# Spreading the next batch's projections over three groups of the first attention in a two-layer decoder kernel

## The chip, the core and the metric

The kernel runs on one core of a Trainium2 chip. A core has TensorE (PE in the profile, its weight loads PEld), VectorE (DVE), ScalarE (ACT), GpSimd (POOL) and SyncE (SP), which here only issues DMAs. The metric is the device time of one execution in microseconds; the time given for a kernel is the median of its runs.

## The reference, cut to what matters

Two decoder layers over `x` of shape (4, 1024, 256), each a self-attention, a cross-attention to 77 context tokens and a feed-forward part, all with a layer norm before and a residual after. The part that matters here is the first self-attention (16 heads of 16, causal, with ALiBi):

```python
x = x + _L0_attn_ref(_layernorm(x), L0_attn_w_attn, L0_attn_w_proj)
...
qkv = x @ w_attn.T
att = einsum(q, k) / sqrt(16) + causal ALiBi bias
y = softmax(att) @ v
return y @ w_proj.T
```

Then follow the cross-attention `_L0_xattn_ref`, the quantised feed-forward `_L0_ffn_ref`, and the second layer.

## The kernel before, in words

The kernel is written as Python generators. Each `yield` ends a step, and `weave(a, na, b, nb)` interleaves two generators so that `na` steps of the one go with `nb` of the other; when one has ended, the rest of the other follows alone. This gives a program order. A list scheduler then places the instructions of each engine: it takes them by readiness and by this order, and may pull later ones forward. Tiles of a tag share a fixed number of buffers (`BUFS`, one where the tag is not named), and a tile waits until a buffer of its tag is released. PSUM has eight banks with fixed duties (`BANKS`): row-maximum matmuls (tag M) and projections (tag Q) share banks 2 and 3, scores (S) have 0 and 1.

The first attention of batch b is `A0(b, after)` (lines 470 to 493). It works through four groups of four heads. In each group the main steps are `a0_main` (20 steps): the scores of a key block against a pair of query blocks (line 401, from the stacks QS and KS in bf16 parts), exp on ScalarE (line 404), and, two steps later, P times V (line 413). Beside them runs a side generator. In groups 0 to 2 it is `nxt`, which loads the next group's stacks (`stacks`, lines 310 to 327, two buffers each of QS and KS) and computes that group's row maxima (`a0_max`, 38 steps, matmul in line 352, reduction on VectorE in line 357). In group 3 it is `after`.

`after` is the front of the next batch, `A0_front(b + 1)`: `qkv` (lines 264 to 308) of 18 steps, then the stacks and the 38 row-maximum steps of its first group. `qkv` loads the weights (`load_w`, lines 256 to 261, 768 KB each into WAh and WAl, one buffer each), and for each half of the 1024 tokens it normalises x on VectorE and GpSimd, transposes it (one step), forms Q and K (four steps, line 288, six matmuls of 512 columns each, split into bf16 parts on ScalarE, VectorE and GpSimd in lines 290 to 293, stored to DRAM as `dr` in lines 296 and 297) and V (four steps, line 303, six matmuls each). For the last batch `after` is the front of the second layer's attention, `A1_front(0)`, with the same 18 steps and its gates.

At the end of `A0` the output is projected, `proj_res` (lines 441 to 460), whose weights also use the buffer WAh. So do `prep_p0` (line 334), which splits that weight once, and `prep_a1`.

Outside, `schedule` (lines 1199 on) weaves A0 of batch b with a side of its own. For batch 0 that is the preparation of weights, in this order: `prep_x(0)`, `prep_p0`, `prep_x(1)`, `prep_f0`; the first eight steps of it go beside the first front. The staging tag `wst`, two buffers, serves all of these. For batches 1 to 3 the side is the cross-attention `XA` of batch b - 1 (two rounds u of heads), the feed-forward `F0` (tanh in line 727, lines 729, 733 and 740 on VectorE), and what is left of the preparation.

Where the 18 projection steps go is set by `GQ`, `NQ` and `NW` (lines 94 and 95): `take(after, 12)` is woven into the side of group 2, the other six stand at the head of group 3, and the side gets 25, 25, 38 and 38 steps for 20 main steps in groups 0 to 3.

## Time and profile before

| | us |
|---|---|
| median of three runs | 2407.63 |
| the runs | 2401.26 to 2417.06 |
| the profiled execution's own time | 2403.86 |
| its span | 2402.1 |
| first attention, first to last score matmul | 102 to 1269 |

The profile is one execution. Busy times of engines are given in us; a row of instructions has its count, its busy time and the mean of one in ns, and the idle time of the engine before it with what ended that. The granted clock of TensorE is given as a share of full speed, the DMA share is the mean busy share of the core's 16 DMA engines. Score matmuls of batch b start at 102, 334, 644 and 948 us.

### The profile page before, as it was taken

Reading aid. Unit: us, or ns where it says so; the run is one execution under the profiler, and the core shown is the slowest. Engines: PE = TensorE matmul, PEld = TensorE weight load, DVE = VectorE, ACT = ScalarE, POOL = GpSimd, SP = SyncE. Lnnn points to the kernel's source line nnn. Section 1 sums busy time; section 2 is a strip of 40 time slices with the busy share of each in tenths; the row PEclk is TensorE's granted clock in tenths of the full one; section 3 lists DMA queues with packets and bytes.
Section 4 is the critical chain, followed back from the end, with each engine's and each line's share of the span. In section 5 each row is a group of like instructions: output and inputs, shape, how many; then the busy total and the mean of one; then the engine's idle time right before and its main releaser. Section 6 shows DMA issues by size and latency. Waiting matters only on the chain.

```text
span 2402.1 us, 51405 instructions
## 1 busy us (share of the span) xinstructions
PE 2150.0 (90%) x19073; PEld 1520.1 (63%) x19110; DVE 1688.9 (70%) x3781; ACT 1638.8 (68%) x4173; POOL 1196.0 (50%) x1942
## 2 busy tenths in 40 slices
PE   6798999998999998899988988889988998899886
PEld 5454457755667655576656766567766767676676
DVE  4666657677666787776765667777866777777775
ACT  4365446676766676565778878987678877887542
POOL 7121303154331352412545458766866787775664
PEclk9899999999999999899989999999999999899997
DMA  8677331224751236222262224412341223542000
GB/s 256 190 206 212 117 90 44 63 57 115 230 143 49 62 105 194 73 73 49 73 188 50 71 71 138 140 38 56 99 116 38 56 80 115 104 99 71 10 10 18
DMA packets 182697, 238.45 MB, mean 99 GB/s; under 512 B 16198, under 2 KB 165846, under 8 KB 175958
## 3 DMA queue, kind: packets, MB, share of 16 engines
q1 hardware_dynamic: 182446, 235.15, 34.9%
q8 instruction: 151, 2.47, 0.4%
q14 instruction: 100, 0.82, 0.1%
HBM read 152.62 MB, written 82.21 MB: 98 GB/s over the span
## 4 chain that ended last, share of the span: by engine, by line
PE 60%; DVE 13%; DMA 8%; ACT 7%; POOL 7%; issue 3%; SPq 1%; POOLq 0%; another core or an unknown queue 0%; ACTq 0%; DVEq 0%
PE T L191 10%; PE W L191 8%; PE O L413 7%; PE Q L191 5%; PE O L927 5%; PE S L401 4%; PE M L352 4%; PE S L898 3%; DVE P L904 2%; DVE s_mt L357 2%; PE W L630 1%; DMA wst<-in_L_xattn_Wq 1%; DMA KS<-c_alk 1%; ACT P L906 1%; PE T L723 1%
## 5 line engine op out<-in xcount | busy, mean ns | idle before, releaser
L357 DVE TENSOR_REDUCE s_mt<-M 128x1 f32<-128x512 f32 (+3 forms) x608 | 386.2, 656 | 135.1 <-PE M L356 97.3
L404 ACT ACTIVATE P<-S 128x512 f32<-128x512 f32 (+1 forms) x640 | 342.0, 562 | 152.3 <-PE S L401 77.0
L906 ACT ACTIVATE P<-P,eps 128x1024 f32<-128x1024 f32 x320 | 343.9, 1080 | 55.5 <-DVE P L904 52.6
L904 DVE TENSOR_REDUCE P<-S 128x512 f32<-128x512 f32 (+1 forms) x480 | 284.8, 611 | 78.2 <-PE S L898 58.6
L352 PE MATMUL M<-KS,QS 108*128 108x512 bf16 (+3 forms) x768 | 225.7, 339 | 47.8 <-DVE s_mt L357 24.6
L898 PE MATMUL S<-QS,KS 96*128 96x256 bf16 (+1 forms) x1280 | 219.4, 270 | 36.6 <-DVE P L904 34.1
L191 PE MATMUL T<-R,xX 128*128 128x352 f32 (+1 forms) x1136 | 246.5, 331 | 4.0 <-ACT E L619 1.4
L401 PE MATMUL S<-QS,KS 110*128 110x256 bf16 (+1 forms) x1280 | 230.4, 267 | 14.7 <-ACT P L404 12.4
L413 PE MATMUL O<-P,V 128*32 128x256 f32 (+1 forms) x2560 | 239.4, 376 | 0.5 <-ACT ot L427 0.2
L622 POOL TENSOR_TENSOR E<-E,s_xsm 128x616 f32<-128x616 f32 x64 | 77.8, 1217 | 323.9 <-DVE s_xsm L620 270.8
L191 PEld LDWEIGHTS T<-R,xX 128*128 128x128 f32 x1136 | 182.9, 190 | 24.1 <-ACT E L619 5.4
L191 PE MATMUL W<-R,xph 128*128 128x256 f32 (+1 forms) x952 | 184.8, 292 | 6.5 <-DVE xpl L180 4.8
L909 POOL TENSOR_TENSOR P<-P,y 128x512 f32<-128x512 f32 x128 | 164.8, 1296 | 31.8 <-ACT y L871 17.0
L619 ACT ACTIVATE E<-T,s_xmx 128x77 f32<-128x77 f32 x512 | 159.3, 333 | 28.1 <-DVE s_xmx L616 26.0
L927 PE MATMUL O<-P,VsJ 128*32 128x128 f32 x3584 | 170.4, 286 | 4.8 <-ACT P L906 3.8
L898 PEld LDWEIGHTS <-KS 96*128 96x128 bf16 x1280 | 102.1, 99 | 110.6 <-issue 88.9
L401 PEld LDWEIGHTS <-KS 110*128 110x128 bf16 x1280 | 106.9, 99 | 102.5 <-issue 58.6
L191 PEld LDWEIGHTS W<-R,xph 128*128 128x128 f32 (+1 forms) x952 | 149.1, 192 | 17.7 <-DVE xpl L180 6.6
L352 PEld LDWEIGHTS <-QS 108*128 108x128 bf16 x768 | 68.1, 99 | 126.5 <-issue 99.2
L191 PE MATMUL W<-R,xpl 128*128 128x256 f32 (+2 forms) x476 | 139.5, 293 | 0.8 <-DVE xpl L180 0.8
L730 POOL TENSOR_TENSOR R<-wst 128x256 f32<-128x256 f32 x128 | 92.9, 736 | 86.0 <-DVE wst L729 80.9
L179 ACT ACTIVATE xph<-W 128x512 fp32r<-128x512 f32 (+2 forms) x180 | 79.1, 457 | 83.1 <-PE W L633 34.0
(351 smaller groups left out, 5662.6 us busy)
## 6 DMA issues: line engine op xcount, KB each, us to landing
QS<-dr SPq DMA_DIRECT2D x144, 192.0 KB
KS<-dr SPq DMA_DIRECT2D x72, 384.0 KB
dr<-qp SPq DMA_DIRECT2D x32, 768.0 KB
MD<-R SPq DMA_DIRECT2D x24, 616.0 KB
UD<-R SPq DMA_DIRECT2D x24, 512.0 KB
R<-MD SPq DMA_DIRECT2D x32, 308.0 KB
X<-in_x SPq DMA_DIRECT2D x16, 512.0 KB
dr<-qp SPq DMA_DIRECT2D x32, 256.0 KB
```

The lines of the kernel that those rows point to most:

```text
L191: nc.tensor.matmul(out, x, y, start=first and n == 0, stop=last and n == len(seq) - 1)
L352: nc.tensor.matmul(Sv[:, x, 0:w], QS[:108, i // 4, hh, i % 4 * 128 : i % 4 * 128 + 128], KS[:108, hh, k0:k1], start=x == 0, stop=not diag ...
L357: nc.vector.tensor_reduce(out, Sv[:, :, 0:w], AX.X, ALU.max)
L401: nc.tensor.matmul(S[:, e, 0:w], st[1][:110, hh, j * 128 : (j + 1) * 128], st[0][:110, q0 // 512, hh, q0 % 512 : q0 % 512 + w], start=e == ...
L404: nc.scalar.activation(P[:, 2 * p : 2 * p + 2, 256 - w :], S[:, :, 0:w], AF.Exp)
L413: nc.tensor.matmul(O[0][hh * 32 : hh * 32 + 32, o + o0 : o + 256], V[j // 4][:, j % 4, h * 17 : h * 17 + 32], P[:, hh, o0:], start=c % 2 = ...
L619: nc.scalar.activation(E[:, n * 77 : (n + 1) * 77], Sv[:, k, :], AF.Exp, bias=mx[:, n : n + 1], accum_out=sm[:, n : n + 1])
L898: nc.tensor.matmul(S[:, e, 0:w], st[r][1][:96, hh, j * 128 : (j + 1) * 128], st[r][0][:96, q0 // 512, hh, q0 % 512 : q0 % 512 + w], start= ...
L904: nc.vector.tensor_reduce(Pv, S[:, :, 0:w].unsqueeze(3), AX.X, ALU.max, apply_absolute_value=True)
L906: nc.scalar.activation(Pw, Pw, AF.Square, bias=self.eps1)
L909: nc.gpsimd.tensor_tensor(Pd, Pd, Ds[r, c][:, j - 2 * c], ALU.mult)
L927: nc.tensor.matmul(Oc[rows, o0 : o0 + 128], lhs, P[:, hh, c0 : c0 + 128], start=j == 2 * c and i == 2 * c, stop=fin and i == 2 * c + 1)
```

## The change

Each of the groups 0, 1 and 2 now takes six steps of `after` beside the 38 row-maximum steps, so that all 18 projection steps are done in the first three groups and group 3's side begins with the stacks and row maxima of the next batch. The side gets 30, 30, 30 and 25 steps for 20 main steps. Nothing that is computed changes.

```diff
-    GQ, NQ = (2, 2, 2, 2), (12, 12, 12, 12)
-    NW = ((25, 25, 38, 38),) * 4
+    NQ = 6
+    NW = (30, 30, 30, 25)
...
         for g in range(4):
             box = []
             side = nxt(g + 1, box) if g < 3 else after
-            if g == self.GQ[b]:
-                side = weave(side, 28, take(after, self.NQ[b]), self.NQ[b])
-            yield from weave(self.a0_main(st, V, y, g, O, pend), 20, side, self.NW[b][g])
+            if g < 3:
+                side = weave(side, 38, take(after, self.NQ), self.NQ)
+            yield from weave(self.a0_main(st, V, y, g, O, pend), 20, side, self.NW[g])
             if g < 3:
                 st = box[0]
```

## The prediction

> **What bounds the kernel now.** I read the page's busy table first, then the busy times stretch by stretch, then what TensorE waited for in the first attention, then two places of the timeline. The times below are of the profiled execution: 2403.86 us by its own time, 2402.1 us of it span; the median of the three timed runs is 2407.63 us, 3.8 us more.

> ```profile
> span 2402.1 us, 51405 instructions
> PE 2150.0 (90%) x19073; PEld 1520.1 (63%) x19110; DVE 1688.9 (70%) x3781; ACT 1638.8 (68%) x4173; POOL 1196.0 (50%) x1942
> ```

> TensorE (PE) carries the span; 252 us of it are idle. The first attention runs from 102 to 1269 us (first to last score matmul, L401); its batches 1 to 3 split at the first and last tanh of F0 (L727):

> ```profile
> core 0: us, PE busy (x) PEld busy (x) DVE busy (x) ACT busy (x) POOL busy (x), PEclk, DMA share, GB/s
> 60.00:75.00 15.00, 8.82 (x51) 6.37 (x51) 5.48 (x10) 4.54 (x10) 2.57 (x3) 0.80 1.06 316
> 102.00:334.00 232.00, 207.70 (x1675) 119.99 (x1673) 142.62 (x269) 131.75 (x276) 53.86 (x53) 0.93 0.57 167
> 334.00:509.00 175.00, 168.66 (x1423) 119.51 (x1422) 120.98 (x281) 110.01 (x407) 37.76 (x53) 0.99 0.24 57
> 509.00:582.00 73.00, 66.02 (x519) 38.36 (x526) 56.98 (x133) 58.51 (x127) 42.30 (x72) 1.00 0.24 74
> 582.00:644.00 62.00, 56.30 (x418) 37.75 (x416) 41.21 (x81) 38.56 (x78) 23.11 (x26) 0.92 0.69 208
> 644.00:842.00 198.00, 195.14 (x1555) 135.53 (x1556) 137.64 (x317) 126.93 (x445) 53.08 (x75) 1.00 0.37 98
> 842.00:923.00 81.00, 75.32 (x566) 44.55 (x573) 62.35 (x144) 60.19 (x133) 40.65 (x65) 0.96 0.35 98
> 948.00:1156.00 208.00, 191.53 (x1505) 131.52 (x1502) 149.26 (x344) 119.51 (x428) 61.13 (x85) 0.95 0.30 82
> 1156.00:1232.00 76.00, 67.61 (x501) 40.40 (x507) 59.11 (x136) 59.42 (x136) 39.34 (x66) 0.96 0.32 102
> 843.00:903.00 60.00, 55.76 (x435) 32.30 (x441) 52.09 (x118) 45.04 (x98) 32.05 (x52) 0.96 0.40 111
> ```

> Per row: PE, weight loads, VectorE (DVE), ScalarE, GpSimd (POOL), granted clock, DMA. The first halves, with XA beside the attention, are solid TensorE (334:509 idles 6.3 us, 644:842 2.9 us). The F0 stretches (509:582, 842:923, 1156:1232) have VectorE at 0.77 to 0.78 and idle 7.0, 5.7 and 8.4 us. Batch 0 (102:334) idles 24.3 us. At 60:75 the DMA engines are full. The waits of TensorE between 102 and 1269 us:

> ```profile
> PE M L352 <- DVE s_mt L357: 22.3, 42, 2.5
> PE M L352 <- DMA KS<-c_alk: 14.0, 4, 6.9
> PE S L401 <- ACT P L404: 12.4, 15, 3.1
> PE M L352 <- DVE yTl L180: 2.8, 4, 1.4
> ```

> Total us, times, longest. Row-maximum matmuls (M) wait for the reduction that frees their PSUM bank, or for the key stack (KS). Two timeline places, the start of the row maxima and the load of batch 1's projection weights:

> ```profile
> 72.38 0.37 PE L352 MATMUL M<-KS,QS 108*128 108x128 bf16 x2 [4.55 <-DMA KS<-dr]
> ```
> ```profile
> 120.06 0.89 SPq L259 DMA_DIRECT2D WAh<-wa  x1
> 126.55 1.24 SPq L260 DMA_DIRECT2D WAl<-wa  x1
> ```

> **The change part by part.** No instruction is added or removed; the two built programs hold the same numbers on every engine. What moves is one batch's 18 projection steps (96 matmuls, 16 transposes, their evacuations, 4 DMA stores, 2 loads of x, 2 of weights) and, because weights and scheduler follow, more than the diff shows.

> *1. The steps themselves.* Eight steps cost 1.39 us of TensorE and eight 0.76 us (six matmuls each, chain of waits at 844 and 911 us), two are transposes of about 1.2 us (8 by 0.15): 19.6 us a batch, 1.1 us a step. Twelve of 18 leave the second half of each attention: 13 us. They land where TensorE idles 1 to 4%, so they cost there what they save here. Net 0, if the second half really becomes shorter; item 4 asks that.

> *2. Start-up, +5 us.* Batch 1's weights load in group 0 now. In the built order SP issues WAl and WAh right after the fourth Wk load of the start-up (some 60 us), no longer at 120 and 127 us; the last QS pieces and the KS pieces of batch 0's first stack stand behind them on SP, and so does the next cross-attention weight load. 2 by 768 KB is 1.57 MB; at the 316 GB/s of 60:75, with the engines full, 5.0 us. The first row maximum already waits 4.55 us for KS, so nothing covers this. Bounds: 0 (if the weight preparation beside it ends later anyway) to +7 (two issues of 0.9 and 1.2 us waited out too). The old place gives nothing back: TensorE was 100% busy there.

> *3. Batch 0 loses its filler, 0 us.* WAh and WAl have one buffer. Batch 1's load now stands before prep_p0, which splits Wproj into the same buffers; so prep_p0 waits until batch 1's 18th step, holding both wst buffers, and prep_x(1) and prep_f0 wait behind it. In the built order prep_x(1)'s matmuls move from 87..164 to 213..289 us of accumulated TensorE work, prep_f0's from 166..196 to 290..331: into the last group of batch 0 and the first of batch 1. On POOL the V memset that waits for batch 0's last P.V (17.5 us at 328 us before) now has half of prep_x(1)'s subtractions behind it; TensorE has proj_res and scores beside them. XA's second round, which reads prep_x(1)'s result, stands 115 us of TensorE work behind it, so it is covered. What it costs: from 102 to about 240 us only the attention and its projections run. Bounds: -14 (all KS waits go, with less DMA beside the stacks) to +16: 140 us at the poorest TensorE share that 60 us of this phase show, 0.78 (927 to 987 us), instead of 102:334's 0.895 are 125.3/0.78 - 140 = +20.6, less 4.5 us, half of batch 0's 9.0 us of KS waits, which lighter DMA should give back. I take 0: attention alone keeps TensorE ahead of ScalarE (1.47 us of matmul a main step against 1.07 us of exp), and the KS waits shrink.

> *4. Second halves, +5 us.* With 20 main steps to 30, 30, 30, 25 side steps, not 25, 25, 38, 38, the side steps left over when a group's main steps are done are 14, 14, 14, 13 instead of 13, 13, 12, 6: in groups 2 and 3, where F0 runs, nine more, most of them row maxima without a score step beside them. Between the first and last tanh of F0 the built order has 24, 35, 30 row maxima before and 47, 46, 43 after; projection steps 10, 14, 13 before, 8, 7, 6.3 after. 47 more reductions by 0.635 us (386.2 us / 608) are +29.8 us of VectorE, 15.7 steps by 0.46 us (8 subtractions of 0.69, 4 of 0.68 in 18 steps) -7.2: +22.6 us in three stretches, 7.5 each. VectorE goes from 57.0, 62.4, 59.1 to about 64.5, 69.9, 66.6 us. The best it held over 60 us is 52.09 of 60 (843:903), 0.87: 74, 80, 77 us against 73, 81, 76. So on the mean it costs +1, in clumps more. Cutting both orders into pieces of 10 us of TensorE work and adding the longest engine of each (mean durations of the rows) gives 1229.8 us before and 1257.8 after for the phase: +28. Bounds: -8 (waits of M and Q on each other's banks, 2.8+2.6+2.5 us, vanish) to +28; taken near the mean's end, because engines slip against each other by more than 10 us and the number of row maxima that stand tightly behind one another does not change (181 and 182).

> *5. End of batch 3.* A1_front(0) ends at 1121 us of TensorE work, before 1125; the wait for its gates (2.1 us) may go: 0, bounds -2 to 0.

> Sum: +5 +0 +5 +0 = +10 us: 2413.9 us for the profiled execution, 2418 against the median. Bounds added up: -24 and +51.

> [...]

> **Rivals.** (a) *Faster*: the KS waits vanish, because each group starts with projections beside it and batch 0's DMA is lighter: -14 us at their four places, and the clock of 102:334 recovers from 0.93 (7% of 232 us, about half of it: -8), with the +5 of item 2: 2386.9, 2391 on the median. For: KS ended 14.0 us of waits. Against: the wait at 72 us grows. It decides if the KS waits left fall below 4 us. (b) *VectorE becomes the bound of the second halves*: item 4 at +28, with +5: 2436.9 plus clock 2, 2443. For: the counts of item 4. Against: 0.87 was reached beside TensorE at 0.93. (c) *Batch 0 starves*: item 3 at +16, with +5: 2425, 2429. For: KS waits of up to 6.9 us even with filler. Against: the step costs in item 3. (d) *Nothing changes*: TensorE is the bound and the order is immaterial: 2408; against it, item 2's queue.

> **How the numbers follow.** Forecast 0.48 (own range 2405 to 2434), (a) 0.13, (b) 0.14, (c) 0.13, (d) 0.12. From (a)'s 2391 to (b)'s 2443, which leave out half of each, some 0.86 lies inside; rounded: 2390 to 2444. About 1% (24 us; 2384 and 2432) is what a measurement of this kernel can tell from no change. Slower by over 1%: (b) 0.14, half of (c) 0.06, the forecast's upper end 0.08: 0.28. Faster: half of (a), 0.07. Within: 0.65.

> **What would show it.** Item 2: both weight loads near 60 us on SP, the first M at 77 to 79 us instead of 72.4. Item 3: no Wk loads between about 110 and 220 us; TensorE at 0.88 to 0.92 there. Item 4: VectorE at 0.85 or more in the F0 stretches, waits of M for L357 above 22.3 us. The forecast is wrong if the first M is on time, if TensorE falls under 0.85 in batch 0, or if the F0 stretches idle more than 30 us together.

## The result and the profile after

The changed kernel takes 2441.06 us (median of four runs, 2437.19 to 2448.28) against 2410.33 us for the kernel before in the same comparison: 1.0148 times as long, with a 95% interval of 1.012 to 1.0176. It is 31 us slower, where +10 was forecast and rival (b) stood at 2443. The profiled execution took 2440.09 us, 2438.3 of it span; the page's first lines:

```profile
span 2438.3 us, 51436 instructions
PE 2181.2 (89%) x19110; PEld 1529.5 (63%) x19110; DVE 1692.4 (69%) x3781; ACT 1641.0 (67%) x4173; POOL 1202.0 (49%) x1942
```

The span is 36.2 us longer, 5.5 more than the medians differ: each profile is one execution, and the one of the kernel before was among its shorter ones. TensorE (PE) idles 257.1 us of the span, 5.1 more than before, and is busy 31.1 us longer with the same matmuls. Of that, 10.5 us are TensorE at half clock, which the record shows as busy time (worked out from the granted clock over the busy time: 88.9 us lost before, 99.4 after). An estimated 4 us are records missing from the trace of before (37 matmuls of 512 columns): taking 37 such records out of the complete trace of after shortens its busy time by 3 to 5 us. The other 16 or so are busy time at the same clock. At full clock a record of each of the larger kinds is as long as before, within 2% (a P.V of 256 columns 391 ns on the mean in both traces, 397 over all clocks), but the records overlap less with their neighbours, so that together they cover more time: those wholly at full clock add up to 5443 us and cover 1967 before, 5432 and 1977 after. The stretches, in the columns shown before, first by batch (first score to first score), then the pieces inside:

```profile
core 0: us, PE busy (x) PEld busy (x) DVE busy (x) ACT busy (x) POOL busy (x), PEclk, DMA share, GB/s
104.10:318.70 214.60, 197.09 (x1593) 110.52 (x1592) 126.79 (x232) 120.23 (x249) 34.56 (x36) 0.94 0.41 112
318.70:660.10 341.40, 308.86 (x2452) 206.17 (x2452) 241.91 (x537) 218.88 (x638) 124.41 (x167) 0.98 0.43 121
660.10:984.20 324.10, 301.21 (x2356) 195.06 (x2355) 232.25 (x530) 209.35 (x615) 106.82 (x154) 0.95 0.41 116
984.20:1298.00 313.80, 292.38 (x2262) 187.72 (x2260) 207.39 (x490) 204.23 (x606) 111.28 (x174) 0.95 0.31 88
...
61.00:82.00 21.00, 17.19 (x70) 13.43 (x71) 10.57 (x21) 5.95 (x13) 2.58 (x3) 0.51 1.05 333
...
523.00:600.00 77.00, 71.23 (x527) 40.67 (x525) 66.49 (x157) 55.70 (x121) 33.95 (x50) 0.96 0.26 72
...
858.00:938.00 80.00, 74.08 (x560) 39.95 (x559) 64.39 (x151) 57.93 (x126) 31.68 (x48) 0.91 0.26 69
938.00:984.00 46.00, 36.54 (x289) 18.78 (x289) 40.56 (x87) 26.44 (x49) 12.93 (x14) 0.81 0.70 223
...
1172.00:1247.00 75.00, 67.84 (x500) 36.97 (x498) 60.56 (x141) 54.33 (x119) 32.41 (x49) 0.93 0.23 71
```

The batches took 231.6, 310.9, 303.9 and 320.6 us before. Batch 0 is 17.0 us shorter and batch 1 30.5 longer, because half of the weight preparation moved from the one to the other; together +13.5. Batch 2 is +20.2, batch 3 -6.8, the start +2.1, all behind the first attention +7.3. The F0 stretches, from first to last tanh 79.2, 80.6 and 75.8 us, are together 3 us longer than before (73.5, 82.0 and 77.0). What has grown in batch 2 is the stretch behind F0, 46 us at a clock of 0.81, partly because it holds more of the batch's matmuls (289 against 215); in the kernel before it was the row

```profile
923.00:948.00 25.00, 22.45 (x215) 11.99 (x212) 20.68 (x45) 17.39 (x33) 4.80 (x7) 0.93 0.85 268
```

Split into waits, clock and busy time at the same clock, batch 2's +20.2 us are +11.8, +6.9 and +1.5. In batches 0 and 1 together the +13.5 are +6.7, -0.6 and +7.4, and behind the first attention the +7.3 are -3.5, +0.7 and +10.1 (the last of the three parts with the missing records). So no one part carries all stretches.

The waits of TensorE over the first attention (104 to 1298 us; total us, times, longest):

```profile
PE M L352 <- DVE s_mt L357: 26.3, 50, 1.7
PE S L401 <- ACT P L404: 13.9, 17, 3.6
PE W L747 <- DVE xph L740: 12.3, 8, 3.2
...
PE M L352 <- DMA KS<-c_alk: 2.6, 1, 2.6
```

The waits of L747 for L740 were half as long in the kernel before (102 to 1269 us):

```profile
PE W L747 <- DVE xph L740: 6.1, 5, 1.7
```

The waits for KS fell from 14.0 to 2.6 us, below the 4 us at which rival (a) was to decide, and nothing of it arrived in the time. In their place are waits of up to 3.6 us, 0.5 to 1.5 us on the mean of a row, spread over many pairs: over the first attention TensorE idles 94.4 us, where it idled 83.7 before. What such waits do to the clock is seen behind F0 of batch 2, where the transposes of the last F0 tiles wait for VectorE (timeline, then the clock of the same place):

```profile
940.43 0.32 PE L352 MATMUL M<-KS,QS 108*128 108x384 bf16 x1 [0.55 <-DVE s_mt L357]
...
942.76 1.03 PE L747 MATMUL W<-identb,xph 128*128 128x128 bf16 x8 [1.95 <-DVE xph L740]
...
948.37 0.59 PE L352 MATMUL M<-KS,QS 108*128 108x256 bf16 x2 [1.04 <-DVE VsJ L384]
...
951.14 1.03 PE L747 MATMUL W<-identb,xph 128*128 128x128 bf16 x8 [1.97 <-DVE xph L740]
```
```profile
928.10:941.70 13.60, 11.48 (x95) 5.48 (x93) 11.70 (x24) 10.88 (x24) 5.21 (x8) 1.00 0.37 93
941.70:955.30 13.60, 9.01 (x47) 5.53 (x48) 10.04 (x28) 4.40 (x6) 1.30 (x2) 0.50 0.89 278
```

TensorE stands at half clock for 13.6 us, four windows of 3.41 us (the last section has these windows): its 9.0 us of busy time there, times the clock, are an estimated 4.5 us of work. The window before, up to 941.66 us, idles 1.85 us, in pieces of 0.45, 0.55 and 0.85 us, of which the last is the first part of the wait for L740. The next three idle 1.40, 1.04 and 1.97 us, the fourth 0.22 us, and behind that the clock is whole again. Last, the start-up. On SP the two weight loads stand ahead of the KS and QS pieces, and the first row maximum (M) comes at 75.11 us, not 72.38:

```profile
57.53 0.89 SPq L260 DMA_DIRECT2D WAl<-wa  x1
58.52 0.42 SPq L259 DMA_DIRECT2D WAh<-wa  x1
...
71.48 1.30 SPq L320 DMA_DIRECT2D KS<-dr  x2
```
```profile
75.11 0.58 PE L352 MATMUL M<-KS,QS 108*128 108x128 bf16 x4 [2.22 <-DMA QS<-dr]
```

### The profile page after: what moved, and what is told of

Read it like the earlier page. It is cut to its first block, busy times and chain, and to the rows that moved or that the text cites. A ratio compares the mean times of both kernels' runs of the same rounds, so it can differ in the third digit from the quotient of the medians.

```text
span 2438.3 us, 51436 instructions
## 1 busy us (share of the span) xinstructions
PE 2181.2 (89%) x19110; PEld 1529.5 (63%) x19110; DVE 1692.4 (69%) x3781; ACT 1641.0 (67%) x4173; POOL 1202.0 (49%) x1942
## 4 chain that ended last, share of the span: by engine, by line
PE 61%; DVE 14%; ACT 7%; DMA 7%; POOL 7%; issue 4%; SPq 1%; POOLq 0%; DVEq 0%; ACTq 0%
PE T L191 10%; PE W L191 8%; PE O L413 7%; PE O L927 5%; PE Q L191 5%; PE S L401 5%; PE M L352 4%; PE S L898 3%; DVE s_mt L357 3%; DVE P L904 2%; PE T L723 2%; DMA wst<-in_L_xattn_Wq 2%; PE W L630 1%; PE W L752 1%; ACT P L906 1%
## 5 line engine op out<-in xcount | busy, mean ns | idle before, releaser
L357 DVE TENSOR_REDUCE s_mt<-M 128x1 f32<-128x512 f32 (+3 forms) x608 | 387.9, 656 | 131.5 <-PE M L356 97.6
L404 ACT ACTIVATE P<-S 128x512 f32<-128x512 f32 (+1 forms) x640 | 339.3, 562 | 133.3 <-PE S L401 79.9
L352 PE MATMUL M<-KS,QS 108*128 108x512 bf16 (+3 forms) x768 | 228.3, 343 | 42.4 <-DVE s_mt L357 28.6
L401 PE MATMUL S<-QS,KS 110*128 110x256 bf16 (+1 forms) x1280 | 230.5, 267 | 18.7 <-ACT P L404 13.9
L927 PE MATMUL O<-P,VsJ 128*32 128x128 f32 x3584 | 176.6, 283 | 6.4 <-ACT P L906 5.0
L401 PEld LDWEIGHTS <-KS 110*128 110x128 bf16 x1280 | 105.9, 99 | 108.0 <-issue 64.9
L352 PEld LDWEIGHTS <-QS 108*128 108x128 bf16 x768 | 69.7, 101 | 118.7 <-issue 95.4
```

The costliest lines, as they stand in the source:

```text
L352: nc.tensor.matmul(Sv[:, x, 0:w], QS[:108, i // 4, hh, i % 4 * 128 : i % 4 * 128 + 128], KS[:108, hh, k0:k1], start=x == 0, stop=not diag ...
L357: nc.vector.tensor_reduce(out, Sv[:, :, 0:w], AX.X, ALU.max)
L401: nc.tensor.matmul(S[:, e, 0:w], st[1][:110, hh, j * 128 : (j + 1) * 128], st[0][:110, q0 // 512, hh, q0 % 512 : q0 % 512 + w], start=e == ...
L404: nc.scalar.activation(P[:, 2 * p : 2 * p + 2, 256 - w :], S[:, :, 0:w], AF.Exp)
L927: nc.tensor.matmul(Oc[rows, o0 : o0 + 128], lhs, P[:, hh, c0 : c0 + 128], start=j == 2 * c and i == 2 * c, stop=fin and i == 2 * c + 1)
```

## The experiments

Unless said otherwise five rounds were taken, and each ratio is to the kernel before in the same comparison.

**Runs 1 to 4: the one weight buffer, and single batches.** Theory Q puts the loss on `prep_p0`, which waits for batch 1's projections to release WAh and WAl; theory V on VectorE in the second halves. Runs 1 and 2 give `prep_p0` the buffers xph and xpl, in the changed kernel and in the kernel before:

```diff
-        self.wp0 = self.prep_w(self.i["L0_attn_w_proj"], 256, "wp0")
+        self.wp0 = self.prep_w(self.i["L0_attn_w_proj"], 256, "wp0", tags=("xph", "xpl"))
```

Runs 3 and 4 make the change only in batch 0, or only in batches 1 to 3 (`new = b in (0,)` or `(1, 2, 3)` chooses between the old and the new lines).

> The changed kernel, but prep_p0 splits Wproj into the buffers xph and xpl instead of WAh and WAl, so that it no longer waits for the last of batch 1's projection steps. Theory Q (the queue behind the one weight buffer): aligned by TensorE work done, the changed kernel loses about 14 us until the middle of batch 1, where the late prep_x(1) and prep_f0 run; with their own buffers they run in batch 0 again and these 14 us return: about 2427 us against 2441, ratio to the kernel before 1.006 to 1.010. Theory V (the second halves, VectorE and F0): the loss sits in the F0 stretches, so nothing returns: 2438 to 2444, ratio 1.013 to 1.016.

> Control: the kernel before with the same other buffers for prep_p0. There prep_p0 stands ahead of batch 1's weight load, so by both theories nothing waits that waited not before: 2405 to 2415 us, ratio 0.998 to 1.002.

> The change (six steps in each of groups 0 to 2, rates 30, 30, 30, 25) in batch 0 alone; batches 1 to 3 as before. Theory Q: the whole buffer queue is in here, so about 14 us of the 31 us: 2424, ratio 1.004 to 1.008. Theory V: batch 0 has no F0 beside it, so nothing: 2410, ratio 0.998 to 1.002.

> The change in batches 1 to 3 alone; batch 0 as before, so prep_p0 and prep_x(1) are on time. Theory Q alone: 2410 us, ratio 0.998 to 1.002. Theory V alone: the whole 31 us, 2441, ratio 1.013. If both hold, each with the part that the alignment by TensorE work shows (14 us by the middle of batch 1, 13 us in the F0 stretches of batches 2 and 3): about 2424, ratio 1.004 to 1.008.

Measured: run 1 2442.70 us (ratio 1.0129, 1.0096 to 1.0161), run 2 2416.31 (1.0039, 1.0017 to 1.006; just over the range expected, so the other buffers cost some 7 us by themselves), run 3 2453.28 (1.0179, 1.0148 to 1.0209), run 4 2438.50 (1.0117, 1.0088 to 1.0146). Run 1 does what Q says where Q says it, batches 0 and 1 by score boundaries:

```profile
106.30:342.50 236.20, 211.75 (x1680) 122.50 (x1679) 151.25 (x279) 130.68 (x276) 54.96 (x53) 0.92 0.56 157
342.50:654.20 311.70, 296.11 (x2355) 194.41 (x2352) 213.09 (x490) 206.43 (x609) 101.13 (x148) 0.97 0.32 88
654.20:990.10 335.90, 303.09 (x2369) 198.70 (x2368) 231.86 (x535) 210.01 (x615) 106.30 (x154) 0.94 0.42 114
```

Batches 0 and 1 together take 547.9 us, against 542.5 before and 556.0 in the changed kernel: 8 of the 13.5 us are back. But batch 2 now takes 335.9, 12 more than in the changed kernel, and the total has not moved. Q falls as the cause of the total. V's numbers fit runs 1 and 4, not run 3: the change in batch 0 alone costs 44 us, in batches 1 to 3 alone 30, in all four 31. The parts do not add up.

**Runs 5 to 8: rates, and VectorE in F0.** Run 5 is the changed kernel with `NW = (32, 32, 32, 32)`, run 6 the kernel before with `NW = ((24, 24, 36, 31),) * 4`. Runs 7 (before) and 8 (changed) shorten the reduction of F0:

```diff
-                nc.vector.tensor_reduce(a[:, 0:1], hp, AX.X, ALU.max, apply_absolute_value=True)
+                nc.vector.tensor_reduce(a[:, 0:1], hp[:, 0:64], AX.X, ALU.max, apply_absolute_value=True)
```

> The changed kernel with the rates (32, 32, 32, 32) in place of (30, 30, 30, 25): six projection steps in each of the first three groups as in the change, but the side steps left over when a group's main steps are done are 12, 12, 12, 6, near the 13, 13, 12, 6 of the kernel before. Theory T (the rates: longer tails of row maxima ahead of the next group's first scores, above all in the last group, 13 for 6): 2400 to 2418, the loss gone. Theory V (VectorE bounds the F0 stretches, since row maxima stand where projections stood): 2433 to 2445, as the changed kernel, since the row maxima stay there. Theory P (where the projection steps stand costs by itself, outside F0): 2433 to 2445 too; told from V by the light pair.

> The kernel before with the rates (24, 24, 36, 31) in place of (25, 25, 38, 38): the placement of the projection steps is the old one, but 14, 14, 14, 13 side steps are left over at the groups' ends, as in the change. Theory T: 2430 to 2445. Theories V and P: 2403 to 2416, the time before.

> The kernel before with F0's reduction for the abs max (L733, 1212 ns, 32 of them) over 64 of the 1024 columns: it leaves out the other 960 columns' part of that max. It takes about 1 us by 8 off VectorE in each F0 stretch and off the tail of each F0 tile. A control for the next run: 2385 to 2405 by every theory.

> The changed kernel with the same reduction over 64 of 1024 columns (the other columns are left out of the max). Theory V: VectorE in the F0 stretches is relieved by 8 us each, so this gains 15 to 24 us more than the control does, and stands 5 to 16 us above it. Theories T and P: it stands 25 to 35 us above the control, as the changed kernel stands above the kernel before.

Measured: run 5 2437.90 us (1.0124, 1.0103 to 1.0146), run 6 2434.38 (1.0106, 1.0088 to 1.0123), run 7 2397.39 (0.9952, 0.9937 to 0.9967), run 8 2440.32 (1.0135, 1.0117 to 1.0153). The old rates' tails do not save the changed kernel (run 5), and longer tails alone cost 26 us (run 6), so T holds one way and fails the other. Runs 7 and 8 tell most. The control gains 11 us, with F0 stretches 5 to 12 us shorter each; the changed kernel gains nothing, although its F0 stretches became 8 to 11 us shorter each, by the first and last tanh. The rows are of run 8, from within 2 us of its first and last tanh:

```profile
526.30:594.50 68.20, 62.02 (x449) 35.54 (x454) 55.72 (x148) 52.53 (x110) 34.19 (x50) 0.97 0.16 55
858.70:927.60 68.90, 62.49 (x465) 35.26 (x472) 56.42 (x147) 53.22 (x114) 34.11 (x50) 0.95 0.17 55
1176.40:1244.10 67.70, 61.17 (x457) 35.07 (x468) 55.67 (x146) 52.64 (x115) 34.47 (x50) 0.95 0.16 56
```

V expected 15 to 24 us more than the control's gain and got some 10 less. VectorE in F0 is not the bound of the changed kernel; that is also rival (b)'s mechanism. What was left is P, that the placement costs by itself, with run 6 (the old placement) against it.

**Runs 9 to 12: the crowded end of batch 2, and the clock by itself.** Runs 9 (changed), 10 (before) and 11 (changed, with run 1's buffers) move a weight preparation:

```diff
-    more = {1: K.prep_x(2), 2: chain(K.prep_a1(), K.prep_f1_up()), 3: K.prep_f1_down()}
+    more = {1: K.prep_x(2), 2: K.prep_a1(), 3: chain(K.prep_f1_up(), K.prep_f1_down())}
```

Run 12 (one execution) replaces the whole decoder by matmul blocks that wait for VectorE copies:

```python
for n in (12, 28):
    for k, v in ((1, 64), (1, 256), (1, 512), (2, 256), (2, 512), (3, 512), (4, 512)):
        for _ in range(16):
            ps = K.p("S")
            nc.tensor.matmul(ps[:, 0:w], K.identb, r[:, 0:w], start=True, stop=True)
            for _ in range(n):
                nc.tensor.matmul(ps, K.identb, base, start=True, stop=True)
            w, a = v, ps
            for x in range(k):
                r = K.t([128, 512], BF if x == k - 1 else F32, "P" if x == k - 1 else "E")
                nc.vector.tensor_scalar(r[:, 0:w], a[:, 0:w], 1.0, None, ALU.mult)
                a = r
```

> The changed kernel with the preparation of the second feed-forward's up weights moved from batch 2's side to batch 3's. In the stretch behind F0 of batch 2 (938 to 984 us of the changed kernel) VectorE is busy 40.7 of 46.1 us, some 20 of it with this preparation, TensorE idles 9.5 us and the clock is 0.81; before, that stretch took 25 us. Theory E (that crowded end holds about 14 of the 31 us): 2424 to 2432, the stretch ends in about 30 us. Theory D (the loss is spread over many short stalls that any other order also makes): 2434 to 2446, what is won there comes back elsewhere.

> The kernel before with the same move, as control. Theory E: 2400 to 2410, since this stretch idles only 2.6 us there. Theory D: 2412 to 2435, since any other order of this kernel loses.

> The changed kernel with both: the projection weights of batch 0's side in buffers of their own (as in the first run of this study, which brought batches 0 and 1 back to within 6 us of the kernel before) and the move of the up weights' preparation. If the losses are local and add up: 2412 to 2425. Theory D: 2434 to 2446.

> No decoder at all (zeros are written, everything is left out): blocks of 12, then of 28 bf16 matmuls of 512 columns, each block waiting for a chain of one to four VectorE copies of the block before, 16 blocks for each of seven chain lengths. Theory C (the granted clock is set by the idle share of windows of 3.41 us: half speed for the next window when about half of one was idle, and held there while more than about 0.15 is): blocks of 12 (2.6 us) with waits under 0.6 us run at 1.0, with waits over 1.2 us at 0.5 to 0.7; blocks of 28 (6 us) hold 1.0 up to waits of 1.3 us and fall to about 0.75 at 2 us and more. [...]

Measured: run 9 2424.68 us (1.0074, 1.0052 to 1.0097), run 10 2394.57 (0.9951, 0.9933 to 0.9969), run 11 2424.34 (1.0075, 1.0051 to 1.0099). The move gains 16 us in the changed kernel, as E says, but 11 in the kernel before, which E did not say: the two stay 30 us apart. E is no cause of the difference. Run 11 lies at the upper end of the range for losses that add up (2412 to 2425), but the buffers add nothing in it (run 11 against run 9), so the local losses do not add up. D, as written, falls too: run 10 is another order and is faster. Run 10 beats both kernels and computes the same. Runs 9 and 10 are the cleanest pair for where the time goes, both with all 19110 matmuls on record:

```profile
span 2423.2 us, 51456 instructions
PE 2167.8 (89%) x19110; PEld 1529.4 (63%) x19110; DVE 1695.0 (70%) x3781; ACT 1640.4 (68%) x4173; POOL 1200.9 (50%) x1942
```
```profile
span 2392.8 us, 51488 instructions
PE 2146.2 (90%) x19110; PEld 1517.3 (63%) x19110; DVE 1691.4 (71%) x3781; ACT 1639.0 (68%) x4173; POOL 1199.7 (50%) x1942
```

Run 9 is first, run 10 second. Idle of TensorE: 255.3 against 246.6, +8.7. Busy: +21.7. Busy time weighted with the granted clock is 2064.2 us in both, so all of that is the clock (103.6 us lost to it against 82.0): in this pair 9 us more of waits went with 22 us more lost to the clock. That the weighted time is the same is particular to this pair: in the six other traces that hold all 19110 matmuls, the changed kernel's among them, it lies between 2055.4 and 2081.8 us.

Run 12 has waits and clock without the decoder. Blocks of 28 matmuls, waits of 1.71 us, then of 2.17 us:

```profile
1062.00:1175.00 113.00, 89.87 (x406) 39.60 (x406) 20.93 (x42) 0.00 (x0) 1.00 0.00 0
1195.00:1337.00 142.00, 113.06 (x406) 45.16 (x404) 26.34 (x54) 0.00 (x0) 0.83 0.00 0
```

One more VectorE copy lengthens the wait by 0.46 us (30.3 against 23.9 us over 14 waits) and the period from 8.13 to 10.26 us, by 2.13. The rest, 1.67, is by an estimate one window of 3.41 us at half speed in each period: that costs 1.71, and the clock of 0.83 takes 1.74 from 10.26 us. Blocks of 12 do the same (4.67 to 6.82 us, clock 1.00 to 0.75). C is right on the step and on the long blocks (0.83 for about 0.75), wrong for short blocks with waits of 1.24 and 1.70 us, which stayed at 1.0 although 30 to 36% of the time was idle, while the long blocks at 0.83 idled 20% of theirs: the idle share of a whole stretch did not set its clock.

**Runs 13 to 16: other placements.** On run 10 as base, with the projection steps of groups 0, 1, 2 as `NQ` and the rest at the head of group 3:

```diff
-            if g == self.GQ[b]:
-                side = weave(side, 28, take(after, self.NQ[b]), self.NQ[b])
+            if g < 3 and self.NQ[g]:
+                side = weave(side, 28 if self.NQ[g] > 6 else 38, take(after, self.NQ[g]), self.NQ[g])
```

Run 13: `NQ = (0, 6, 6)`, run 14 `(0, 0, 18)`, run 15 `(6, 6, 0)`, run 16 `(0, 0, 6)`.

> On the tenth kernel of this study (2394.6): 0, 6, 6 projection steps in groups 0 to 2 and six at the head of group 3, rates 25, 30, 30, 38, so six steps stand one group earlier. Theory B (local balance: the sum over pieces of 10 us of TensorE work of the engine busiest in each, taken from the built orders, is 6 us higher, and 15 us higher went with 30 us before): 2404 to 2412. Theory L (the last group loses its projections; row maxima alone there): 2390 to 2402, since group 3 keeps its six.

> The same base with all 18 projection steps in group 2 and none in group 3, rates 25, 25, 43, 32. Theory B (the sum over pieces is 0.6 us lower): 2388 to 2400. Theory L: 2412 to 2427, since group 3 has no projection left, as in the change.

> The same base with 6, 6, 0 steps in groups 0 to 2 and six at the head of group 3, rates 30, 30, 25, 38. Theory B (the sum over pieces is 16 us higher; VectorE is the longest there where six steps went into group 0, beside the start and end of the cross-attention): 2417 to 2432. Theory L: 2392 to 2405.

> The same base, the other way: only six steps in group 2 and twelve at the head of group 3, rates 25, 25, 30, 43. Theory B (the sum over pieces is 6 us lower): 2380 to 2392. Theory L: 2385 to 2398. Both: no slower than the base.

Measured: 2461.80 us (1.0228, 1.0203 to 1.0254), 2428.59 (1.0086, 1.0062 to 1.0109), 2436.44 (1.0116, 1.0091 to 1.014) and 2433.27 (1.0104, 1.008 to 1.0129): 67, 34, 42 and 39 us above run 10. (Run 10 was measured in another comparison, whose kernel before took 1.7 us less.) B fails on run 13 (2404 to 2412 expected), 14 (2388 to 2400) and 16 (2380 to 2392) and misses run 15 by 4 us, so the sum over pieces is no measure of this either; L fails on 13, 15 and 16 and misses run 14 by 2 us. Even the opposite of the change, projections later than before, loses. In all four runs the rates change together with the placement, and rates alone cost 26 us in run 6: what placement alone costs is not separated.

All pairs that differ in the weave of the first attention alone, old placement and rates against others (the split is of the profiled executions, one of each kernel; what is left of the span's difference, 0 to 22 us, is TensorE records that overlap less at the same clock, and missing records. From run 10 to run 13, for one, the 2048 P.V of 256 columns take 394 and 395 ns on the mean, but cover 202.2 and 216.6 us):

| pair | difference of medians, us | idle of TensorE, us | lost to the clock, us |
|---|---|---|---|
| before, changed | +31 | +5.1 | +10.5 |
| the same, own buffers (runs 2, 1) | +26 | +6.5 | +17.7 |
| the same, light reduction (7, 8) | +43 | +18.3 | +9.3 |
| the same, preparation moved (10, 9) | +30 | +8.7 | +21.6 |
| before, runs 3, 4 (some batches) | +44, +30 | +16.9, +14.9 | +25.4, +8.8 |
| before, run 5 | +30 | +7.1 | +17.0 |
| before, run 6 (rates alone) | +26 | +4.6 | +18.3 |
| run 10, runs 13, 14, 15, 16 | +67, +34, +42, +39 | +19.4, +11.7, +17.6, +23.0 | +34.1, +18.1, +8.5, +4.6 |

Edits that leave this weave alone went the other way or cost little: run 2 +7, run 7 -11, run 10 -11.

The executions of one kernel differ in their clock. Over the 51 executions of the kernel before in the comparisons of runs 1 to 16 (2397.8 to 2425.4 us, mean granted clock 0.960 to 0.945) the time rises by 1.5 us for each 0.001 that the clock falls, with a correlation of -0.82. The mean of that clock is 0.954 in these, 0.952 in the four executions of the changed kernel, 0.958 in run 10 and 0.950 in run 9. By that slope the clock is worth an estimated 3 us of the 31 in the first pair and 12 of the 30 in the second, less in both than the split of single executions gives.

## Why the prediction was wrong, point by point

The step that failed is that the same instructions take TensorE the same time: item 1's "Net 0", with the clock left out of the sum. The sum's +10 is waits for other engines and queues. Measured were +5.1 us of idle time and +31.1 us of busy time in the profiled pair, +8.7 and +21.7 in the clean pair (runs 10 and 9). The second failure is item 4, whose +5 us stood in the wrong place. None of the prediction's own signs of being wrong appeared: the first M was late, TensorE was 0.92 busy in batch 0, and the three F0 stretches idle 18.9 us together, not over 30. The loss lay where no sign looked.

*Item 1, the steps, 0:* runs 9 and 10 do the same 2064.2 us of clock-weighted TensorE work with the steps in either place, but the kernel before and the changed one do not: 2061.2 and 2081.8 us, of which the missing records explain an estimated 4. So net 0 is not shown.

*Item 2, start-up, +5:* right in mechanism, the loads stand where forecast (57.5 and 58.5 us on SP), and the first M still waits for a DMA. The size was 2 to 3 us, within its bounds: the first M came 2.7 us later (77 to 79 was forecast, 75.1 measured), the first score 2.1. The wait itself became shorter (2.22 us against 4.55), while from 61 to 82 us the clock was 0.51, against 0.84 in the same stretch before; up to the first score TensorE idles 2.0 us less and loses 5.7 us more to the clock.

*Item 3, batch 0's filler, 0:* batch 0 itself did not starve (TensorE 0.93 busy from 110 to 220 us, where 0.88 to 0.92 was forecast, and no Wk load on SP from 90 to 260 us) and is shorter by the moved preparation; but batches 0 and 1 together lost 13.5 us, inside the bounds of -14 to +16 and far from the value taken. Run 1 gives 8 of it back by taking away the wait for WAh and WAl, and batch 2 then loses 12 more.

*Item 4, second halves, +5:* this step failed in place and size: batches 2 and 3 together are +13.4 us. F0 is only 3 us longer in the three stretches together; VectorE stood at 0.86, 0.80 and 0.81 there, not at 0.85 or more throughout, and lightening it (run 8) bought nothing. The waits of M for its reduction rose from 22.3 to 26.3 us as said. The loss of batch 2 sat behind F0, in a stretch that the prediction did not price: 25 us before, 46 after.

*Item 5, end of batch 3, 0:* the 2.1 us wait for the gates is gone from batch 3, as the item allowed; the batch is 6.8 us shorter, more than its bounds, with 7.9 us less of waits.

*The clock:* the sum counted waits and left the clock out, though the row of 582:644 stood at 0.92, by an estimate 5 us lost of its 62, with no wait there over 1.4 us. In the change's own pair the clock took 10.5 of 36.2 us, in the clean pair 21.6 of 30.4, in the other pairs 4.6 to 34.1. It is the largest part in seven of the twelve pairs, but not in the change's own, where busy time at the same clock is larger (about 16 us).

*Rivals:* (a)'s KS waits did vanish and the kernel is still slower, so "it decides if they fall below 4 us" was wrong: waits that go in one place came back in others. (b) had the number (2443) by a cause that run 8 excludes, so its number is luck; the 2 us of clock in it are shown by no run, and 10.5 were measured in the change's own pair. (c) falls with the batches' rows, batch 0 being shorter, and (d) with the result.

What stays open: why the old weave has fewer waits, and TensorE records that overlap more, than nearly every other that was tried. The list scheduler's order shifts everywhere when one rate changes, and no single pair of engines, batch or buffer holds the difference in all of these kernels. That the constants of this weave suit this one order would explain it, but is only argued. Holding TensorE busy through the waits, to see the clock's share alone in the decoder, was not tried.

## What to carry to other kernels

When TensorE is the bound at 90%, price a reordering by the short waits that it makes and not only by the work that it moves, and add something for the clock: over the twelve pairs above 154 us more of waits went with 194 us more lost to the clock, though in single pairs it is 0.2 to 4 times the waits. A wait that an edit removes is a gain only if no other pair of engines waits in its place: compare the time at equal TensorE work, not single stretches. Split a profile's difference into idle time, clock and busy time at the same clock, and do not take the last as fixed. In an order made by a scheduler from weights, try small changes of the weights in both directions before believing a mechanism, and try each edit on the old kernel as a control: here it showed three causes to be none, and gave the faster version.

## What the runs showed of the hardware

| idle share of TensorE in a window | next window at half clock, from a window at full clock (10477) | from a window at half clock (1072) |
|---|---|---|
| under 0.1 | 0.00 | 0.09 |
| 0.1 to 0.2 | 0.00 | 0.72 |
| 0.2 to 0.3 | 0.01 | 1.00 |
| 0.3 to 0.4 | 0.17 | 1.00 |
| 0.4 to 0.5 | 0.50 | 1.00 |
| 0.5 to 0.6 | 0.91 | 1.00 |
| over 0.6 | 1.00 | 1.00 |

So in these traces, of the full-clock windows that idled 0.4 to 0.5 of their 3.41 us (1.4 to 1.7 us), 0.50 were followed by half clock, and of those that idled 1.7 to 2.0 us 0.91. Several short waits went with it no less: at an idle share of 0.4 to 0.5, of the 95 full-clock windows with no wait of 1 us or more within them 0.78 were followed by half clock, and of the 121 with over three quarters of the idle time in one wait 0.24. From half clock, 0.91 of the windows that idled under 0.1 (0.34 us) were followed by full clock, 0.28 of those that idled 0.1 to 0.2, and hardly any that idled more. The windows behind F0 of batch 2 agree: those that idled 1.85, 1.40, 1.04 and 1.97 us were each followed by half clock, the one with 0.22 us by full clock, so the clock stood at 0.50 for 13.6 us. In run 12 blocks of 28 matmuls ran at 1.00 with waits of 1.71 us and at 0.83 with waits of 2.17 us. In eight of the twelve pairs, the change's own among them, more time was added through the clock than through the waits themselves.
